# Shifted rows of the last image fetched between partitions of SBUF, second averages and bank copies moved up, and TensorE's results stored on SP's queue

## The chip, the cores and the metric

One core of one Trainium2 chip runs the whole program. Its engines work at the same time and meet through semaphores: TensorE (PE, with the weight loads PEld), VectorE (DVE), ScalarE (ACT), GpSimd (POOL) and SyncE (SP, which here only issues transfers). POOL issues transfers too. The metric is the device time of one execution, in microseconds (us); less is better.

## The reference, cut to what matters

The input is 16 images of 384 channels and 32 x 32 pixels, in float32. Layer 0 is attention over the 1024 pixels, layer 1 a 7 x 7 convolution of each channel by itself; both have a group normalization (32 groups of 12 channels, no affine) ahead of them and are added to their input.

```python
x = x + attention(gn(x), w_qkv, w_proj, b_proj)     # 8 heads of 48
w_sym = (w + rot90(w,1) + rot90(w,2) + rot90(w,3)) * 0.25
x = x + depthwise_conv7x7(gn(x), w_sym, pad=3)
def gn(v):                                          # per image, per group of 12 channels
    return (v - mean(v)) / sqrt(var(v) + 1e-5)
```

## The kernel before, in words

The channels lie on partitions in three tiles of 128 (`NK = 3`, index `k`). Image after image, TensorE makes q and k (line 489) and v (line 515), then per pair of heads the scores (560), whose exponentials ACT takes (568), and the sums over v (580), and the projection (641; for the last image in parts, 685). The result, with the residual, is x1. DVE does the convolution of the image before beside it, by folding (`fold_ops`, lines 771 to 876): it uses the left-right symmetry of the weights, so that it adds shifted copies (`sides`), collects them by row offset (`rows_e`, `rows_o`), and adds these to x1 in place.

Three of the 48 tiles of the convolution go to TensorE: `PE_TILES` are (14, 2), (15, 2) and (15, 1) (image, k). Only (15, 0), called `LAST`, is left to DVE at the end. A tile on TensorE goes through these steps:

- `conv_begin` (712): ACT copies x1 into xn with even and odd rows apart (line 725). For image 15 the values are not normalized yet: the scale is put in at the end and the shift comes in as a "border" term.
- `conv_store` (961): SP writes xn to `xd` in DRAM, two planes of 16 + 3 rows, with rows of zeros around them that POOL wrote once in `conv_prepare` (904, at about 500 us).
- `conv_load` (972): for each half `a` of the channels (64), SP issues four loads from `xd`; each fills one group of 16 channels with eight row-shifted copies each, 128 partitions in all (`sh`). `loads` (1459) says when.
- `conv_on_pe` (992): 7 taps by 4 groups of matmuls per half, into PSUM (`ps_conv`). The tap matrices are made on DVE from `wsh`, which POOL gathered in `conv_prepare`.
- `conv_take` (1019): ACT copies the bank to SBUF (`rows`, line 1022). `conv_perm` (1024): TensorE puts the rows back in channel order by two matmuls a half (1031, `ps_rows`); ACT copies out with the scale (1046; for image 14 without, 1050); POOL adds it to x1 by an accumulating transfer (1052), and the sum is stored (1054), on SP for half a tile and on POOL for a whole one.

The order of the work is written out by hand: a small planner keeps two clocks, `clock` for TensorE and `vclock` for DVE. `after(wait, cost, f)` puts DVE work in a queue of due times; `catch_up(t)` issues due work and taps of the folding until `vclock` is at `t`. Each engine then runs what it was given strictly in that order, and a wait holds everything behind it on that engine.

The end of the last image stands in `fast_finish` (1510) and `fast_end` (1534). After the last projection `fast_end` begins both TensorE tiles, lets ACT take the moments of the three channel tiles, and lets TensorE average them over groups in two steps: `st.average` of the means (line 363), then `spread_of` on DVE (374 to 376), then `st.average` of the squares, then `scale_of` (380 on DVE, and a power on POOL, 381), then `factors` (1578: `shift_of` on DVE, 384; nine activations for three border tiles on ACT, 1593; three accumulating transfers on POOL, 1596). From then on DVE can put the scale into `LAST` (line 804) and end it with two half stores on SP (880). Between these steps stand the pieces of TensorE's convolution, `pe_conv`.

At the program's end each engine loads a flag (`again`, 1677) and branches around a general version of the kernel that isn't needed (1678); then all meet in a barrier (1722).

Of the kernel before, what the change touches and what calls it, by code (L numbers as in the profile page):

```python
# [45 lines left out]
def kernel(  # L46
# [100 lines left out]
    def run(general):  # L147
        tag = "g" if general else "f"
        with ExitStack() as stack:
# [32 lines left out]
            def flat(t):  # L182
                return t.rearrange("p h n -> p (h n)")
# [521 lines left out]
            def by_rows(t):  # L705

                return t.rearrange("p (m q w) -> p q m w", q=2, w=W)
# [4 lines left out]
            def conv_begin(st, b, k, engine=None):  # L712
                name = f"xn1_{b}_{k}"
                if general:
                    xn1s[b, k] = npool.tile([P, N], F32, tag="xn1", name=name)
                elif b == B - 1:
                    xn1s[b, k] = flat(epool.tile([P, 2, HALF], F32, tag="e", name=name))
                else:
                    xn1s[b, k] = tpool.tile([P, N], F32, tag="t", name=name)
                if general:  # L720
                    st.apply(xn1s[b, k], x1s[b, k], k, engine)
                else:
                    dst = xn1s[b, k].rearrange("p (q m w) -> p q m w", q=2, w=W)
                    if b == B - 1:
                        nc.scalar.copy(dst, by_rows(x1s[b, k]))
                    else:
                        st.apply(dst, by_rows(x1s[b, k]), k)

            def conv_tap(b, k, dy, dx):
                (oy, iy), (ox, ix) = region(dy, dx)  # L730
# [10 lines left out]
            def grid(t):  # L741
                return t.rearrange("p (h w) -> p h w", w=W)
# [153 lines left out]
            NG = P // CG  # L896
            PLANE = (H // 2 + PAD) * W

            def inputs(i):

                first = (1 - i % 2) * RI // 2 + i // 2
                return slice(first, first + (CG - 1) * RI + 1, RI)

            def conv_prepare():
# [5 lines left out]
                with nc.allow_non_contiguous_dma(reason="small, once"):  # L910
                    nc.gpsimd.dma_start(
                        w_rows[:, :, KS : (KS + 1) * KS], wsym.rearrange("p k i j -> p k (i j)")
                    )
                    none = zero[:, 0 : NK * KS].rearrange("p (k t) -> p k t", k=NK)
                    nc.gpsimd.dma_start(w_rows[:, :, 0:KS], none)
                    nc.gpsimd.dma_start(w_rows[:, :, (KS + 1) * KS :], none)
                    for n, k in enumerate(PE_K):
                        for i in range(RI):
                            nc.gpsimd.dma_start(
                                wsh[inputs(i), n].rearrange("p g t d -> p g (t d)"),  # L920
                                bass.AP(
                                    w_d.tensor,
                                    w_d.offset + (k * P * (KS + 2) + i) * KS,
                                    [[(KS + 2) * KS, CG], [CG * (KS + 2) * KS, NG], [1, 2 * KS]],
                                ),
                            )
                for bk in PE_TILES:
                    xd = dconv.tile([P, 2 * PLANE], F32, tag=f"x_{len(xds)}", name=f"xd_{len(xds)}")
                    xds[bk] = xd

                    for lo, n in ((0, 1), (H // 2 + 1, 2), (H // 2 + 3, 2), (2 * PLANE // W - 1, 1)):
# [40 lines left out]
            def conv_load(b, k, a):  # L972

                t = qkpool.tile([P, 2, N], F32, tag="qk", name=f"sh_{b}_{k}_{a}")
                t = t.rearrange("p a n -> p (a n)").rearrange("p (g n) -> p g n", n=HALF)
                xd = xds[b, k]

                for i in range(NG // 2):
                    nc.sync.dma_start(
                        t[:, i],  # L980
                        bass.AP(
                            xd.tensor,
                            xd.offset + (a * NG // 2 + i) * CG * 2 * PLANE,
                            [[PLANE, 2 * CG], [W, RI // 2], [1, HALF]],
                        ),
                    )
                shs[b, k, a] = t


# [34 lines left out]
            def conv_perm(b, k, a):  # L1024
# [29 lines left out]
                queue.dma_start(  # L1054
                    out[b, k * P + part.start : k * P + part.stop].rearrange("p h w -> p (h w)"), dst
                )

            def exact_step(u, i):
# [406 lines left out]
            def conv_piece(rows=True):  # L1465
# [44 lines left out]
            def fast_finish(b):  # L1510
# [3 lines left out]
                for o in range(NK):  # L1514
# [19 lines left out]
            def fast_end(b):  # L1534
# [41 lines left out]
            ends = {}  # L1576
# [149 lines left out]
```

## Time and profile before

| | us |
|---|---|
| median of 3 runs | 2852.77 (2851.55 to 2854.41) |
| the profiled execution, its own time | 2858.37 |
| its span, first to last instruction | 2856.6 |
| PE busy in the span | 2831.3 (99%) |
| DVE, ACT, POOL busy | 2079.9, 1664.2, 264.1 |
| granted TensorE clock, mean | 0.995 |

The page has the busy time of each engine, forty slices of the span, the transfers by queue, the chain of work that ended last and the costliest groups of instructions. The trace behind it answers questions: the chain in order of time, who waited for whom in a stretch, the instructions of one line, and the busy time, the clock and the DMA rate of any stretch. Times in it count from the span's start. "A <- B" says that A waited for B; q after an engine's name is its sequencer.

### The profile page before, as it was taken

How to read it: one execution, taken by the hardware profiler on the slowest of the kernel's cores; microseconds unless marked ns; L12 is line 12 of the kernel's file. 1: busy time of each engine (PE TensorE's matmuls, PEld its weight loads, DVE VectorE, ACT ScalarE, POOL GpSimd, SP SyncE). 2: the span in 40 equal slices, each digit the busy share in tenths (PEclk: the TensorE clock that was granted, in tenths of full speed). 3: DMA queues.
4: the chain of work that ended last, by engine and by line, in shares of the span. 5: the costliest groups of instructions: out<-in, count | busy, mean ns of one | idle time of the engine just before them, and what ended most of it. 6: DMA issues, size and time to landing. Idle time of an engine off the chain costs nothing.

```text
span 2856.6 us, 46038 instructions
## 1 busy us (share of the span) xinstructions
PE 2831.3 (99%) x19342; PEld 1116.2 (39%) x19342; DVE 2079.9 (73%) x2261; ACT 1664.2 (58%) x1951; POOL 264.1 (9%) x418
## 2 busy tenths in 40 slices
PE   9999999999999999999999999999999999999996
PEld 5344343433434344343433434334343433434332
DVE  4503968959598695977959598595977959598786
ACT  2637647475574746647475574756647476574733
POOL 3201011310101001010010100001010010100001
PEclk9999999999999999999999999999999999999998
DMA  6622131211212112030211212112130121202225
GB/s 242 189 37 49 34 74 28 55 50 44 64 32 58 45 39 67 27 81 24 51 50 44 64 32 49 52 37 64 34 81 24 44 57 42 66 25 50 62 74 149
DMA packets 76153, 170.49 MB, mean 60 GB/s; under 512 B 31680, under 2 KB 33728, under 8 KB 74400
## 3 DMA queue, kind: packets, MB, share of 16 engines
q0 software_dynamic: 33360, 110.93, 15.2%
q1 hardware_dynamic: 42576, 56.52, 7.2%
q8 instruction: 154, 2.52, 0.4%
q14 instruction: 63, 0.52, 0.1%
HBM read 117.09 MB, written 28.68 MB: 51 GB/s over the span
## 4 chain that ended last, share of the span: by engine, by line
PE 97%; issue 1%; DMA 1%; POOL 0%; ACT 0%; SPq 0%; POOLq 0%; DVE 0%
PE ps_s L560 31%; PE acc L580 31%; PE ps_qk L489 17%; PE ps_v L515 9%; PE ps_proj L641 8%; PE warm L1396 0%; PE ps_proj_last L685 0%; PE ps_conv L1007 0%; DMA sh<-xd 0%; DMA x<-border 0%; DMA x<-conv 0%; PE ps_st_x L363 0%; POOL x L1052 0%; DMA xd<-xn 0%; PE ps_rows L1031 0%
## 5 line engine op out<-in xcount | busy, mean ns | idle before, releaser
L568 ACT ACTIVATE e<-ps_s 128x1024 f32<-128x1024 f32 x1024 | 1021.8, 1030 | 446.5 <-PE ps_s L560 445.2
L560 PE MATMUL ps_s<-qk 48*64 48x512 f32 x8192 | 1033.7, 589 | 0.0
L580 PE MATMUL acc<-e,v 64*64 64x512 f32 x8192 | 1033.0, 588 | 0.0
L780 DVE TENSOR_TENSOR side<-padded 128x1024 f32<-128x1024 f32 x270 | 329.3, 1220 | 339.4 <-ACT padded L751 339.3
L783 DVE SCALAR_TENSOR_TENSOR rows_e<-side,even,rows_e 128x1024 f32<-128x1024 f32 x405 | 509.7, 1274 | 85.7 <-ACT rows_e L762 84.1
L580 PEld LDWEIGHTS acc<-e,v 64*64 64x64 f32 x8192 | 307.0, 132 | 573.6 <-issue 573.4
L560 PEld LDWEIGHTS ps_s<-qk 48*64 48x64 f32 x8192 | 305.5, 132 | 576.8 <-issue 526.2
L489 PE MATMUL ps_qk<-x,wqk 128*128 128x512 f32 x1152 | 502.5, 595 | 0.0
L489 PEld LDWEIGHTS ps_qk<-x,wqk 128*128 128x128 f32 x1152 | 218.1, 190 | 277.8 <-issue 273.0
L799 DVE TENSOR_TENSOR x<-x,rows_e 128x992 f32<-128x992 f32 (+2 forms) x270 | 311.1, 1152 | 0.0
L799 DVE TENSOR_TENSOR x<-x,rows_o 128x928 f32<-128x928 f32 (+2 forms) x265 | 304.2, 1148 | 3.0
L496 ACT COPY qk<-ps_qk 128x1024 f32<-128x1024 f32 x96 | 97.2, 1012 | 318.5 <-PE ps_qk L489 318.5
L515 PE MATMUL ps_v<-wv,x 128*128 128x384 f32 x768 | 252.6, 486 | 0.0
L641 PE MATMUL ps_proj<-o,wp 128*128 128x512 f32 x540 | 234.2, 592 | 0.0
L535 ACT COPY v<-ps_v 64x384 f32<-64x384 f32 x256 | 121.6, 475 | 122.4 <-PE ps_v L515 119.8
L515 PEld LDWEIGHTS ps_v<-wv,x 128*128 128x128 f32 x768 | 145.9, 190 | 108.2 <-issue 14.3
L783 DVE SCALAR_TENSOR_TENSOR rows_o<-side,odd,rows_o 128x1024 f32<-128x1024 f32 x135 | 172.8, 1280 | 1.6
L783 DVE SCALAR_TENSOR_TENSOR x<-side,even,x 128x1024 f32<-128x1024 f32 x135 | 172.6, 1279 | 0.0
L886 POOL DMA_DIRECT2D out<-x x44 | 24.6, 558 | 1590.3 <-DVE x L799 1590.2
L641 PEld LDWEIGHTS ps_proj<-o,wp 128*128 128x128 f32 x540 | 102.6, 190 | 126.2 <-issue 117.7
L649 ACT ACTIVATE x<-ps_proj,bp 128x1024 f32<-128x1024 f32 x45 | 50.2, 1115 | 167.5 <-PE ps_proj L641 167.5
L762 ACT ACTIVATE rows_e<-padded,even 128x1024 f32<-128x1024 f32 x135 | 146.8, 1167 | 0.0
(165 smaller groups left out, 1044.5 us busy)
## 6 DMA issues: line engine op xcount, KB each, us to landing
x<-in_x POOLq DMA_DIRECT2D x90, 512.0 KB, 5.4
inv<-inv SPq DMA_DIRECT2D x126, 256.0 KB
out<-x POOLq DMA_DIRECT2D x46, 512.0 KB, 3.0
xs<-in_x POOLq DMA_DIRECT2D x42, 512.0 KB, 6.5
qk<-qk POOLq DMA_DIRECT2D x96, 128.0 KB, 4.1
sh<-xd SPq DMA_DIRECT2D x24, 256.0 KB
o<-o SPq DMA_DIRECT2D x180, 32.0 KB
x<-in_x SPq DMA_DIRECT2D x6, 512.0 KB
```

The costliest lines, as they stand in the source:

```text
L489: nc.tensor.matmul(ps[:, h, :], lhsT=wqk[:, k, s, t, :], rhs=xns[b][:, k, h * HALF : (h + 1) * HALF], start=(k == 0), stop=(k == NK - 1),)
L496: nc.scalar.copy(halves(qks[u][:, s, :]), ps)
L515: nc.tensor.matmul(ps[:, j, 0:C], lhsT=xns[b][:, k, t * P : (t + 1) * P], rhs=wv[:, k, :], start=(k == 0), stop=(k == NK - 1),)
L535: nc.scalar.copy(dst[:, :, 0 : HEADS // 2 * (D + 1)].rearrange("p k (h d) -> p k h d", d=D + 1)[:, :, :, 0:D], src.rearrange("p k (h d) -> ...
L560: nc.tensor.matmul(ps[64 * c : 64 * c + 64, a, :], lhsT=qk[r, 1, 64 * kb : 64 * kb + 64], rhs=qk[r, 0, h * HALF : (h + 1) * HALF], start=True,
L568: nc.scalar.activation(es[n], ps, AF.Exp, scale=SCALE)
L580: nc.tensor.matmul(accs[a][64 * j : 64 * j + 64, :], lhsT=v[rows, kb, c : c + 64], rhs=e[rows, j, :], start=(kb == 0), stop=(kb == 2 * NT ...
L641: nc.tensor.matmul(ps[:, h, :], lhsT=wp[:, t, o * P : (o + 1) * P], rhs=os_[b, t // 2][:, t % 2, h * HALF : (h + 1) * HALF], start=(t == 0 ...
L762: nc.scalar.activation(grid(rows_e[dy - 1]), padded_view(i), AF.Identity, scale=even[:, k, dy, 0:1],)
L780: vec.tensor_tensor(grid(sides[n]), padded_view(i, j), padded_view(i, -j), op)
L783: vec.scalar_tensor_tensor(dst, src, w, dst, ALU.mult, ALU.add)
L799: vec.tensor_tensor(dst, dst, src, op)
```

## The change

It acts on the convolution on TensorE and on the order of the work after the last attention.

- The copy of (15, 2) and (15, 1) goes into planes with rows of zeros inside SBUF (`late["planes", k]`, in the memory of `v`, which is no longer needed; POOL sets the zero rows by six memsets in `fast_finish`). ACT makes it in two copies of 512 columns instead of one of 1024. `conv_store` isn't called for image 15, and the two `xd` tensors of these tiles are gone.
- `conv_load` issues eight transfers a half instead of four, one for each row shift. For image 15 they go from the planes to `sh`, from SBUF to SBUF on SP; for (14, 2) from `xd` in DRAM, now on POOL. Channels lie in another order in `sh`, so the gather of `wsh` (32 transfers instead of 16) and `perm` are laid out to match. POOL's zero rows for `xd` are four transfers instead of twelve.
- `loads(2)` stands right behind the copies in `fast_end`, and another `loads(1)` ahead of the first piece of (15, 2).
- For image 15 ACT takes a bank right after its last tap, in `conv_piece`.
- In `fast_end` the second average stands one piece of convolution after the first (now four taps, before three taps and a permutation); the permutation of (14, 2) comes behind it. DVE's due times are 1.5, 1.5 and 4.0 instead of 2.5, 2.2 and 4.5.
- The last half tile (15, 1, a = 1) is added to x1 on DVE from PSUM (`conv_add`, two instructions of 64 x 512), not by ACT and an accumulating transfer.
- All stores of TensorE's tiles are issued on SP.

```diff
                 elif b == B - 1:
-                    xn1s[b, k] = flat(epool.tile([P, 2, HALF], F32, tag="e", name=name))
+                    xn1s[b, k] = late["planes", k]
+                    for q in range(2):
+                        nc.scalar.copy(
+                            grid(xn1s[b, k][:, (q + 1) * W + q * PLANE :][:, 0:HALF]),
+                            by_rows(x1s[b, k])[:, q],
+                        )
+                    return
...
+            NONE = ((0, 1), (H // 2 + 1, 4), (2 * PLANE // W - 1, 1))
...
-                            nc.gpsimd.dma_start(
-                                wsh[inputs(i), n].rearrange("p g t d -> p g (t d)"),
...
+                            for a in range(2):
+                                half = slice(a * NG // 2, (a + 1) * NG // 2)
+                                row = (KS + 2) * KS
+                                nc.gpsimd.dma_start(
+                                    wsh[inputs(i), n, half].rearrange("p g t d -> p g (t d)"),
...
-                for bk in PE_TILES:
+                for bk in PE_TILES[0:1]:
...
-                        perm[:, row].rearrange("p (g c) -> p g c", c=CG),
+                        perm[:, row].rearrange("p (c g) -> p g c", c=CG),
...
-                for i in range(NG // 2):
-                    nc.sync.dma_start(
-                        t[:, i],
...
+                half = slice(a * P // 2, (a + 1) * P // 2)
+                for i in range(RI):
+                    lo = (1 - i % 2) * PLANE + i // 2 * W
+                    if (b, k) in xds:
+                        nc.gpsimd.dma_start(t[inputs(i)], xds[b, k][half, lo : lo + HALF])
+                    else:
+                        nc.sync.dma_start(t[inputs(i)], xn1s[b, k][half, lo : lo + HALF])
                 shs[b, k, a] = t
...
+                if (b, k) == PE_TILES[-1] and a == 1:
+                    after(4.0, 1.5, lambda: conv_add(b, k, part))
+                    return
...
-                dst = x1s[b, k][part]
-                nc.gpsimd.dma_start(dst, t[part], accum_op=ALU.add)
-                queue = nc.sync if part.stop < P else nc.gpsimd
-                queue.dma_start(
-                    out[b, k * P + part.start : k * P + part.stop].rearrange("p h w -> p (h w)"), dst
+                nc.gpsimd.dma_start(x1s[b, k][part], t[part], accum_op=ALU.add)
+                store(b, k, part)
+
+            def conv_add(b, k, part):
+                s = ends["st"].sc[part, k, 0:1]
+                for q in range(2):
+                    dst = by_rows(x1s[b, k][part])[:, q]
+                    nc.vector.scalar_tensor_tensor(
+                        dst, grid(pss[b, k][part, q, :]), s, dst, ALU.mult, ALU.add
+                    )
+                store(b, k, part)
+
+            def store(b, k, part):
+                nc.sync.dma_start(
+                    out[b, k * P + part.start : k * P + part.stop].rearrange("p h w -> p (h w)"),
+                    x1s[b, k][part],
                 )
...
                 if last == KS:
                     loads(1)
+                    if b == B - 1:
+                        conv_take(b, k, a)
                     perms.append((b, k, a))
 
             def conv_rows():
-                for p in perms:
-                    conv_take(*p)
                 while perms:
...
                 check_vector()
+
+                planes = v.rearrange("p k c -> p (k c)")
+                for n, k in enumerate(PE_K):
+                    late["planes", k] = t = planes[:, n * 2 * PLANE : (n + 1) * 2 * PLANE]
+                    for lo, rows in NONE:
+                        nc.gpsimd.memset(t[:, lo * W : (lo + rows) * W], 0.0)
...
                     conv_begin(st, b, k)
-                    conv_store(b, k)
-                    pe_conv.extend(((b, k, 0, 0, KS), (b, k, 1, 0, 3), (b, k, 1, 3, KS)))
+                    pe_conv.extend(((b, k, 0, 0, KS), (b, k, 1, 0, 4), (b, k, 1, 4, KS)))
+                loads(2)
...
                     conv_piece(False)
+                for p in perms:
+                    conv_take(*p)
+                loads(1)
                 conv_piece(False)
                 catch_up(clock)
                 mean, var = st.first
                 st.average(late["masks"], 0, mean)
                 clock += 1.6
-                after(2.5, 0.6, lambda: st.spread_of(mean, var))
+                after(1.5, 0.6, lambda: st.spread_of(mean, var))
                 first = [perms.popleft() for _ in range(2)]
-                for p in first:
-                    conv_take(*p)
                 conv_piece(False)
-                for p in first:
-                    conv_perm(*p)
                 catch_up(clock)
                 st.average(late["masks"], NK, st.d)
                 clock += 1.6
-                after(2.2, 0.2, st.scale_of)
-                after(4.5, 0.4, lambda: factors(st))
+                after(1.5, 0.2, st.scale_of)
+                after(4.0, 0.4, lambda: factors(st))
+                for p in first:
+                    conv_perm(*p)
                 conv_piece(False)
-                catch_up(clock + 2.0)
+                catch_up(clock)
```

More of the change, by code (lines that the diff above doesn't have):

```diff
@@ L723, in conv_begin @@
                     dst = xn1s[b, k].rearrange("p (q m w) -> p q m w", q=2, w=W)
[L724 to L727, printed above, removed]
+                    st.apply(dst, by_rows(x1s[b, k]), k)
             def conv_tap(b, k, dy, dx):
@@ L918, in conv_prepare @@
                         for i in range(RI):
-                            nc.gpsimd.dma_start(
-                                wsh[inputs(i), n].rearrange("p g t d -> p g (t d)"),
[L921 to L926, printed above, removed]
-                for bk in PE_TILES:
+                            for a in range(2):
[3 more added lines that the diff above has]
+                                    wsh[inputs(i), n, half].rearrange("p g t d -> p g (t d)"),
+                                    bass.AP(
+                                        w_d.tensor,
+                                        w_d.offset + (k * P + a * P // 2) * row + i * KS,
+                                        [[NG // 2 * row, CG], [row, NG // 2], [1, 2 * KS]],
+                                    ),
+                                )
+                for bk in PE_TILES[0:1]:
                     xd = dconv.tile([P, 2 * PLANE], F32, tag=f"x_{len(xds)}", name=f"xd_{len(xds)}")
                     xds[bk] = xd
-                    for lo, n in ((0, 1), (H // 2 + 1, 2), (H // 2 + 3, 2), (2 * PLANE // W - 1, 1)):
+                    for lo, n in ((NONE[0], (NONE[1][0], 2), (NONE[1][0] + 2, 2), NONE[2])):
                         nc.gpsimd.dma_start(xd[:, lo * W : (lo + n) * W], zero[:, 0 : n * W])
@@ L975, in conv_load @@
                 t = t.rearrange("p a n -> p (a n)").rearrange("p (g n) -> p g n", n=HALF)
-                xd = xds[b, k]
-                for i in range(NG // 2):
-                    nc.sync.dma_start(
-                        t[:, i],
[L981 to L986, printed above, removed]
+                half = slice(a * P // 2, (a + 1) * P // 2)
[5 more added lines that the diff above has]
+                        nc.sync.dma_start(t[inputs(i)], xn1s[b, k][half, lo : lo + HALF])
                 shs[b, k, a] = t
@@ L1050, in conv_perm @@
                     nc.scalar.copy(by_rows(t), src)
-                dst = x1s[b, k][part]
-                nc.gpsimd.dma_start(dst, t[part], accum_op=ALU.add)
-                queue = nc.sync if part.stop < P else nc.gpsimd
-                queue.dma_start(
-                    out[b, k * P + part.start : k * P + part.stop].rearrange("p h w -> p (h w)"), dst
+                nc.gpsimd.dma_start(x1s[b, k][part], t[part], accum_op=ALU.add)
[6 more added lines that the diff above has]
+                        dst, grid(pss[b, k][part, q, :]), s, dst, ALU.mult, ALU.add
+                    )
+                store(b, k, part)
[3 more added lines that the diff above has]
+                    x1s[b, k][part],
                 )
```

## The prediction

> **What bounds the kernel now.** I read the page first, then the chain in order of time, the waits after 2770 us, the clock by stretches, and the last instructions.
>
> ```profile
> PE 2831.3 (99%) x19342; PEld 1116.2 (39%) x19342; DVE 2079.9 (73%) x2261; ACT 1664.2 (58%) x1951; POOL 264.1 (9%) x418
> ...
> PE 97%; issue 1%; DMA 1%; POOL 0%; ACT 0%; SPq 0%; POOLq 0%; DVE 0%
> ```
>
> TensorE sets the time up to the last image's projection, and nothing of the change touches its order there. So only the end can move. The chain in order of time (start, length, what), from the copies of x1 on:
>
> ```profile
> 2785.34 2.79 DMA xd<-xn
> ...
> 2790.13 6.48 DMA sh<-xd
> ...
> 2796.65 7.58 PE ps_conv L1007 x48
> ...
> 2811.70 5.78 DMA x<-conv
> ...
> 2822.75 6.15 DMA x<-border
> ...
> 2830.90 4.49 issue
> ...
> 2836.85 3.53 issue
> ...
> 2841.20 4.52 issue
> ```
>
> Here transfers carry the end. The three "issue" pieces are POOL waiting for a landed sum before it may store it, then for ACT, then for the last sum. The waits between 2770 and 2858 us (total, times, longest):
>
> ```profile
> POOL out L1054 <- DMA x<-conv: 14.2, 3, 5.2
> ...
> PE ps_rows L1031 <- ACT rows L1022: 4.0, 2, 3.3
> DVE d_x L374 <- PE ps_st_x L363: 3.1, 1, 3.1
> DVE sc_x L384 <- POOL sc_x L381: 2.5, 1, 2.5
> ...
> PE ps_conv L1007 <- DMA sh<-xd: 2.2, 1, 2.2
> ...
> DVE x L804 <- DMA rest<-border: 0.8, 1, 0.8
> ```
>
> TensorE's two gaps cost twice: the stretch after each ran at half clock (by stretch: busy time of each engine, then as the last three figures clock, DMA share and GB/s).
>
> ```profile
> 2797.95:2801.37 3.42, 3.42 (x24) 1.04 (x20) 3.42 (x4) 2.13 (x6) 0.00 (x0) 0.50 1.00 331
> ...
> 2825.26:2828.67 3.41, 3.41 (x11) 0.76 (x11) 2.57 (x3) 0.35 (x1) 0.00 (x0) 0.50 1.02 192
> ```
>
> DVE ends at 2836.83, TensorE at 2838.90. The rest is closing. By line, the instructions of SP's stores, of the branch and of the barrier:
>
> ```profile
> L880 SPq DMA_DIRECT2D out<-x x2: 1448/1654/1860, 2841.9 to 2843.8; - x2
> ...
> L1678 POOLq COMPARE_BRANCH  x1: 58/58/58, 2846.7 to 2846.7; - x1
> L1678 POOLq INC_SWDGE_SEM  x1: 1196/1196/1196, 2850.4 to 2850.4; - x1
> ...
> L1722 POOLq DRAIN  x3: 50/98/4152, 2851.6 to 2856.3; - x3
> ```
>
> POOL closes last: store issued 2845.73 to 2846.29, branch 2846.7, first instruction behind it 2849.9, 1.2 us, a drain of 4.15, barrier, end at 2856.6: 10.3 us behind its store. SP branches at 2845.3 and is at work again at 2848.6.
>
> [...] the accumulating half tiles moved 94 GB/s at DMA share 1.00 (2841.6 to 2844.4), the trace shows no plain copy from half the partitions to another place in SBUF. [...]
>
> **The change part by part.**
>
> *Early work.* `conv_prepare`: 16 more gathers, 8 fewer zero rows, at 0.53 us each: 4.2 us on POOL, which ends there at 521.3 and next has work at 530.8. Nothing, with 9.5 us of cover. The 16 loads of (14, 2), 0.55 to 0.9 us each on POOL, come near 2713 and 2723 where POOL waits from 2716.7 to 2770.9; their matmuls start at 2776.3. A store of (14, 0) may issue some us later; nobody waits. Nothing; without cover up to 14 us. SP loses 8 issues there. The six memsets fall behind 2771.4, before ACT's copies at 2784.3.
>
> *First wait.* Two ACT copies of 512 columns, by the 0.58 us of a bank copy (128 x 512), end at about 2785.4 like the one of 1.05. Gone: the store to DRAM, 2.79 us. SP then issues 8 loads instead of 4. Not shown before; the nearest are the old loads at 0.60 us (0.51 to 0.99, twice the bytes), 0.65 with the gap. Low end 0.5, high end the 1.86 of a half store. I take 0.65: 8 x 0.65 = 5.2, issued by 2790.6; landing about 2 us later, 2792.6. [...] TensorE is done with (14, 2) at 2794.5, so its wait of 2.17 goes, and with it 1.55 of half clock (7.58 against 6.03 for 56 records, by 32 in 3.46 at full clock elsewhere). (15, 2, 0) ends at 2800.55 instead of 2804.2. All 32 loads take 32 x 0.65 = 21 us, to 2806.2; the last half is needed at 2819.8.
>
> *Averages.* First average 1.65: 2802.2. DVE comes to `spread_of` one tap (1.1) earlier, at 2801.8, and waits about 0.5 instead of 3.1; done 2802.8. TensorE: four taps 3.45 (2805.65), second average 1.65 (2807.3), the permutation 1.9 (2809.2). The power on POOL stands behind the accumulating transfer of (14, 2): ACT copy 1.0 (2810.3), 0.3, issue 0.88 (2811.5), power 0.91: 2812.4. Before, the power also stood behind a store that waited 5.2 us; it ended at 2819.25. So the factors come 6.8 us sooner. DVE gets there after six taps, at 2810, and waits 2.5.
>
> *DVE's end.* From `spread_of` to its last tap DVE worked 30.4 - 2.45 - 0.84 = 27.1 us; with the moved tap 28.2. So 2802.8 + 28.2 + 2.5 = 2833.5. The border term lands near 2820 and is used at 2823: no wait. Then `conv_add`: two instructions, by the 0.74 us of the 128 x 512 sum from PSUM (line 699), 1.45: 2834.95.
>
> *TensorE's end.* 2809.2, three taps 2.6 (2811.8), (15, 1, 0) 6.05 (2817.9), permutation 1.9 without wait or half clock, since the banks are taken (2819.8; was 2828.2), four taps 3.45, permutation 1.9, three taps 2.6 (2827.75), bank copy and permutation 2.65: 2830.4 instead of 2838.9. It is ahead of DVE.
>
> *Sums and stores.* Three border transfers from 2814.5 on land as before 5 to 7 us after issue, (15, 2) is summed at about 2823 to 2829, its half of (15, 1) at 2826.5 to 2832, each landing followed by a store on SP that waits there: SP's order is (14, 2), (15, 2), (15, 1, 0), the two halves of `LAST`, (15, 1, 1). The last three wait for DVE at 2832.8, 2833.5 and 2835. What is late next, if the sum of (15, 1, 0) lands after 2833, is all three. The last is issued by 2835.6 at 0.6 each; the 1.45 and 1.86 of before came while a half tile was being accumulated, which is over then. With those prices it is 2836.7.
>
> *Closing.* SP branches at 2835.6, 3.3 us, eight plus twelve waits 1.4, barrier and end 0.8: 2841.1. POOL's last issue is at 2827.4, and with the landing of that sum (2832) ahead of the 1.2 and 4.15 its closing is over at 2837.7, so the drain of 4.15 leaves the path.
>
> Sum against the profiled span: 2841.1 - 2856.6 = -15.5 us. The profiled execution's own time, 2858.37, is 1.77 above its span and 5.6 (0.2%) above the median; I carry the difference over: 2852.77 - 15.5 = 2837.3.
>
> **Rivals.**
>
> 1. *The closing stays with POOL.* If POOL's closing starts only after the last store's issue, as now, the end lies 10.3 behind that: 2835.6 + 10.3 = 2845.9, -10.7: 2842.1. For: the drain is the last thing in the trace. Against: nothing links it to SP.
> 2. *The first loads land late.* The first matmul needs all eight now, not one of four. Landing at 2797 leaves the wait and the half clock: (15, 2, 0) ends at 2804.6, 4.0 later, DVE's wait at `spread_of` grows by as much and moves all behind it: 2845.1, so 2841.3. For: in the old kernel the fourth load took 6.48 us. Against: that one stood behind two stores and three other loads, this one behind seven loads of half the size.
> 3. *Slower: copies inside SBUF are dear.* With d us per load on SP, the last lands at 2785.4 + 32d + 2, and behind it lie 8.0 of taps and permutation, 2.65, 1.55, 0.7 and 5.5 of closing: the span ends at 2805.8 + 32d. At d = 0.65 this doesn't bind; from 1.10 it sets the end, from 1.59 it is slower than before, from 1.77 by over 0.2%. At the 1.86 of the half store it gives 2865.3, so 2861.5. [...] Against: old loads moved 300 GB/s (2788 to 2791) at 0.60 us[...].
> 4. *It doesn't move.* DVE is still held by the power, or several small delays add up; d near 1.6: 2852.
>
> **How the numbers follow.** Forecast 0.63; rival 1 0.12; rival 2 0.12 (with the other delays of a few us); rival 3 0.08 in all, of which 0.06 over the 0.2%; rival 4 0.03, and 0.02 for gains under 0.2%. 0.2% is about 5.7 us, what a measurement of this kernel can tell from none: faster means under 2847.1. Faster 0.63 + 0.12 + 0.12 + 0.02 = 0.89 (the 0.02 of rival 3 below 1.59 counts as same); same 0.05; slower 0.06. Low end: DVE without any wait ends 3.0 sooner, 2834.3, less run noise 2834.0; the high end takes in rivals 1 and 2 with 1.1 for dear half stores and run noise, 2845.
>
> **What would show it.** No TensorE gap before the first (15, 2) matmul and no half clock until 2830; loads at 0.5 to 0.7 us each; power done near 2812; `LAST` done near 2833.5, the sum from PSUM behind it; POOL's drain over before SP's last store lands. Wrong it is if loads cost over 1.1 us, the power stays behind 2815, or the drain still comes last.

## The result: 11 us faster, and the profile after

The changed kernel takes 2842.75 us (median of 7 runs, 2841.55 to 2846.19), the kernel before beside it 2853.82 (7 runs, 2851.20 to 2857.96): a ratio of 0.9962 [0.9951, 0.9974], 11.1 us less. The forecast was 2837.3 in a range of 2834 to 2845, 15.5 us less.

The profiled execution of the changed kernel took 2846.19 us with a span of 2844.1. From its page, busy time and the chain that ended last:

```profile
PE 2828.3 (99%) x19342; PEld 1117.4 (39%) x19342; DVE 2081.4 (73%) x2263; ACT 1663.4 (58%) x1952; POOL 268.6 (9%) x444
...
DVE 0%; issue 0%; DVEq 0%
```

In what the view could follow of the chain, back to 2824.3, only DVE stands; TensorE and transfers have left it. Its last pieces in order of time (start, length, what) are the end of `LAST` and the sum from PSUM:

```profile
2833.54 0.66 DVE x L800
2834.20 0.20 DVEq L1701
2834.40 0.15 DVE x L800
2834.55 0.34 issue
2834.89 1.43 DVE x L1064 x2
```

The view of the chain leaves out the issuing of transfers, and there is one more step on SP. DVE is done at 2836.32, SP's last store is issued from 2837.86 to 2838.36. Its queue is late because the store of (15, 1)'s first half waits there until 2834.6 for its landed sum, and the two half stores of `LAST` come behind it. The first line is from SP's own waits between 2825 and 2845 us, the others from the engines' waits between 2772 and 2846 us (total, times, longest):

```profile
SPq L1070 <- DMA x<-conv: 15.6, 2, 14.0
...
DVE sc_x L384 <- POOL sc_x L381: 1.7, 1, 1.7
...
PE ps_rows L1034 <- ACT rows L1025: 0.7, 1, 0.7
```

There is no wait of TensorE for `sh` and none of DVE for `ps_st_x`. POOL no longer waits for a landed sum to store it; that wait now stands on SP. What POOL still waits for is hidden in this view: its queue stands from 2818.6 to 2824.3 and from 2824.8 to 2828.5 (the line of L1057 below) until two border transfers have landed, ahead of the sums into the same tiles. This execution's end lies 2.8 us later in time than that of the forecast's profile; the two stretches of time that ran at half clock there are at full clock here (columns as before; clock, DMA share and GB/s last):

```profile
2797.95:2801.37 3.42, 3.42 (x40) 1.01 (x32) 3.38 (x4) 3.36 (x10) 0.00 (x0) 1.00 0.43 147
...
2825.26:2828.67 3.41, 3.14 (x26) 0.68 (x24) 3.38 (x4) 1.31 (x2) 0.41 (x1) 1.00 1.02 193
```

Half clock comes only at 2833.9, behind TensorE's last matmul (2831.0). By line, the instructions of SP's loads and stores, of POOL's waits ahead of its sums, of POOL's drain, and SP's first instructions behind the branch (times one by one in ns, then first and last start):

```profile
L989 SPq DMA_DIRECT2D sh<-v x32: 531/595/1446, 2788.2 to 2809.9; - x32
...
L883 SPq DMA_DIRECT2D out<-x x2: 532/1163/1794, 2835.4 to 2836.0; - x2
...
L1057 POOLq EVENT_SEMAPHORE  x2: 3659/4702/5746, 2818.6 to 2824.8; - x2
...
L1746 POOLq DRAIN  x3: 50/98/4111, 2836.1 to 2843.8; - x3
...
L1702 SPq EVENT_SEMAPHORE  x8: 17/17/17, 2841.9 to 2842.4; - x8
```

The loads cost 0.70 us each (21.7 us between the first and the 32nd). POOL's long drain runs from 2836.05 to 2840.16, and SP comes out of its branch only at 2841.9: the closing is on SP, and POOL's lies beside it.

For what follows, "the end" is the time from the start of the last matmul of line 685 (the last projection) to the span's end; this leaves out what happened earlier. It was 72.05 us in the profile that the forecast was made from and is 56.78 here: 15.27 less, where 15.5 was forecast. Yet the median of the runs moved by 11.1. The experiments first ask where those four microseconds are, then what each part of the change is worth.

### The profile page after: what moved, and what is told of

It reads as the page before. It is cut to its first block, busy times and chain, and to the rows that moved or that the text cites. A ratio compares the mean times of both kernels' runs of the same rounds, so it can differ in the third digit from the quotient of the medians.

```text
span 2844.1 us, 46108 instructions
## 1 busy us (share of the span) xinstructions
PE 2828.3 (99%) x19342; PEld 1117.4 (39%) x19342; DVE 2081.4 (73%) x2263; ACT 1663.4 (58%) x1952; POOL 268.6 (9%) x444
## 5 line engine op out<-in xcount | busy, mean ns | idle before, releaser
L515 PEld LDWEIGHTS ps_v<-wv,x 128*128 128x128 f32 x768 | 145.9, 190 | 108.2 <-issue 14.3
```

The source lines that it names most:

```text
L515: nc.tensor.matmul(ps[:, j, 0:C], lhsT=xns[b][:, k, t * P : (t + 1) * P], rhs=wv[:, k, :], start=(k == 0), stop=(k == NK - 1),)
```

## The experiments

Ends and marks in us from the start of the last matmul of line 685, one profiled execution each (DVE and SP: end of their last work; SP's closing left out):

| kernel | first average starts | DVE | SP | span's end |
|---|---|---|---|---|
| before, first profile | 19.64 | 52.31 | 60.75 | 72.05 |
| before, second | 16.61 | 48.98 | 57.40 | 68.41 |
| before, third | 15.94 | 48.75 | 56.99 | 68.19 |
| before, fourth | 16.48 | 48.11 | 55.45 | 67.13 |
| changed, first | 14.48 | 49.00 | 51.05 | 56.78 |
| changed, second | 14.48 | 49.00 | 50.35 | 55.83 |

**The kernel before, again.** No edit.

> The kernel before, once more. Measured from the last matmul of line 685 to the end, its profiled execution took 72.05 us and the changed kernel 56.78: 15.3 less, as forecast, while the medians differ by only 11. Theory A [...]: the two half-clock stretches in the profiled end (1.55 + 1.9 us) are not in every execution; another profile shows an end of 68.5 to 70.5 us with one of them or none, and times spread in steps of about 1.7 us. Theory B (the change made the part before the end slower): the end is again near 72, and the missing 4 us must lie ahead of it.

2858.77 us (13 runs) against 2857.83 (23): 1.0004 [0.9996, 1.0013]. The end was 68.41 us, 3.6 shorter than in the first profile and 0.09 below the range of theory A. TensorE's weight loads waited for `sh` twice, 1.8 us together (3.1 in one wait in the first profile, where the matmuls stood still for 2.17), and the stretch behind was at full clock. Two further executions of the same kernel were profiled at the close to learn which end is usual.

> The kernel before as it is, one look. Two profiles of its end so far gave 72.05 us (TensorE's first gap one wait of 2.17 us, and the stretch behind it at half clock) and 68.41 (the gap in two waits of about 1 us, no half clock behind it). If the long end is usual, this look gives 71 to 73 and a half-clock stretch near 14 us behind the last matmul of line 685; if it is the rarer one, 67.5 to 69.5 without. The forecast's sum was made against the long end; the medians (11 us) fit the short one.

> The same again, for the same question: which of the two ends of the kernel before is usual. 71 to 73 with a half-clock stretch behind the first gap, or 67.5 to 69.5 without.

2854.57 and 2852.02 us (one run each; the kernel before beside them 2857.72), ends of 68.19 and 67.13, the second 0.4 below the range named. So the long end is one of four. In all four the first load of (15, 2) is issued 3.7 us after the mark and the next seven at the same times to 0.02 us; in the first profile alone TensorE then stands still for 2.17 us, in the others its matmuls pause for less than 0.15 us there. The loads landed later in that execution, and why stays open. The waits of the fourth profile from 2775 to 2855 us:

```profile
PE ps_rows L1031 <- ACT rows L1022: 3.0, 2, 2.3
...
PEld ps_conv L1007 <- DMA sh<-xd: 1.7, 2, 1.1
```

and its clock over the whole of TensorE's end (columns as above):

```profile
2796.00:2831.00 35.00, 32.02 (x249) 11.38 (x242) 32.55 (x36) 12.33 (x22) 7.15 (x9) 1.00 0.58 143
```

Here the second gap of 2.3 us cost no half clock at all, whereas the 2.17 us of the first profile did. The second and the third profile have a gap of 3.1 and 3.4 us there, and one half-clock stretch of 3.4 us behind it.

Where the clock changes can be read in the traces. In the first profiles of both kernels every stretch between two changes lasts a whole multiple of 3.413 us, to 0.01 us (3.41, 23.89, 3.41 and 13.65 us from 2797.95 on in that of before). With the time laid off in such steps from the trace's first clock entry, the step ahead of the first profile's half-clock stretch, then the two that hold the fourth profile's gap (columns as above):

```profile
2794.54:2797.95 3.41, 1.30 (x16) 0.56 (x20) 3.38 (x4) 3.35 (x8) 0.00 (x0) 1.00 0.98 329
...
2813.81:2817.22 3.41, 2.67 (x28) 0.65 (x20) 3.38 (x5) 3.39 (x8) 1.30 (x2) 1.00 0.21 84
2817.22:2820.63 3.41, 1.87 (x8) 0.71 (x8) 2.67 (x3) 1.97 (x4) 1.66 (x2) 1.00 1.02 192
```

In the first, TensorE worked for 1.30 of 3.41 us, and the next 3.41 ran at half clock; ahead of the same profile's second half-clock stretch it had worked for 0.87 (2821.84 to 2825.26). In the fourth, the border between two steps cuts the gap into 0.74 and 1.54 us; 2.67 and 1.87 us of work are left, and the clock stays full. So in these executions half clock went with how much work the gap left in one step, and not with the gap's length alone. At what amount of work it sets in was not measured, and these few cases don't show a rule.

**The kernel before, with TensorE kept busy in both gaps.**

```diff
+            def keep_warm(dst, n):
+                m = late["masks"].rearrange("p b c -> p (b c)")
+                for _ in range(n):
+                    nc.tensor.matmul(dst, lhsT=m[:, 0:P], rhs=m[:, 0:HALF], start=True, stop=True)
...
+                if (b, k, a, first) == (B - 1, PE_K[0], 0, 0):
+                    keep_warm(dst, 2)
...
+                    if (b, k) == (B - 1, PE_K[0]):
+                        keep_warm(pss[b, k][:, 0, :], 3)
```

> The kernel before with two idle matmuls ahead of the first taps of (15, 2) and three ahead of its permutation, into banks that the next matmul clears, so that TensorE's two gaps are filled; nothing is left out. The two profiles of the kernel before took 72.05 us for the end with two half-clock stretches in it and 68.41 with one. If the half clock is what differs: no such stretch until TensorE's last matmul and an end of 66 to 67.5 us. If something else differs between the two profiles: the end stays at 68.4 or more.

2855.41 us against 2858.58: 0.9992 [0.9984, 1.0]. There was no half clock before 2838, and yet the end was 68.73 us, no shorter than the usual one. The idle matmuls took more than the gap: the first average started at 18.28 instead of about 16.5. TensorE ended 0.7 us earlier than in the second profile, POOL's and SP's work at the same time as there (58.22 and 57.32 us against 58.11 and 57.40), with 14.3 us of POOL's waits for landed sums. What TensorE won behind the second gap a transfer took back: POOL's sum of (15, 2) waited 4.4 us for a landed border transfer, where it had waited for ACT in the second profile. How much of that the later average caused isn't separated, and the test can't price the first gap, since its fillers cost what they saved.

**The changed kernel, again.** No edit.

> The changed kernel as it is, a second time, on the chip of the following run. My theory: its end (from the start of the last matmul of line 685 to the span's end) has no TensorE gap of over 1 us, [...] and it repeats at 56.78 us within 0.7, where that of the kernel before gave 72.05 and 68.41 in two executions. The ratio to the kernel before is then 0.9955 to 0.9968 (10 to 13 us). The rival, that the 56.78 was as much a chance as the 72.05, expects an end of 59 or more, or a half-clock stretch after the last projection.

2842.94 us against 2853.62: 0.9966 [0.9952, 0.9979]. The end was 55.83; TensorE's, DVE's, ACT's and POOL's work ended at the same 43.73, 49.00, 41.74 and 42.5 us as in the first profile, and the clock was full to TensorE's last matmul. That is 0.25 below the range named, by 0.7 us of one store on SP (below). What was a chance is the long end of before; that of the changed kernel repeats in its two profiles. In the second, TensorE worked for 31.30 of the 32 us from 2795 to 2827; its longest gap is 0.70 us. Between the two profiles of the changed kernel lie 4.9 us of span, and 3.9 of them had passed by the last projection: the first matmul for q and k of image 1 starts at 177.6 in one and 173.7 in the other, behind 10.2 and 3.4 us of half clock at the start (11.1 to 21.4 and 13.8 to 17.2 us).

**Only the rows of image 15 through DRAM again.** All else stays as changed, with eight loads a half.

```diff
-                    xn1s[b, k] = late["planes", k]
-                    for q in range(2):
-                        nc.scalar.copy(...)
+                    xn1s[b, k] = flat(epool.tile([P, 2, HALF], F32, tag="e", name=name))
+                    dst = xn1s[b, k].rearrange("p (q m w) -> p q m w", q=2, w=W)
+                    nc.scalar.copy(dst, by_rows(x1s[b, k]))
...
-                for bk in PE_TILES[0:1]:
+                for bk in PE_TILES:
...
-                        nc.sync.dma_start(t[inputs(i)], xn1s[b, k][half, lo : lo + HALF])
+                    queue = nc.gpsimd if b < B - 1 else nc.sync
+                    queue.dma_start(t[inputs(i)], xds[b, k][half, lo : lo + HALF])
...
+                    conv_store(b, k)
```

> The changed kernel, but the shifted rows of image 15 go through DRAM again (store, then eight loads a half). If the fetch inside SBUF is what took the first wait away: TensorE waits 2 to 3 us for the first loads again, perhaps with a half-clock window behind it, and the end is 2 to 4.5 us longer than the 56.8 of the changed kernel. If the fetch is hidden either way and the other edits carry the gain: within 0.7 us of it.

2850.58 us, 0.9966 [0.9954, 0.9978]; end 61.63, 4.9 to 5.8 us longer than the changed kernel's two, more than the 2 to 4.5 expected. The waits from 2787 to 2851 us bring back what was forecast to go:

```profile
PE ps_conv L1005 <- DVE x L783: 2.4, 1, 2.4
DVE d_x L374 <- PE ps_st_x L363: 2.3, 1, 2.3
```

(The profile names a DVE line as TensorE's releaser; the matmuls that wait are the first of (15, 2), and the only new work ahead of them is the store to DRAM and the loads from it: the first load is issued 3.69 us after the mark, as in the kernel before, where the changed kernel issues it at 0.91.) A half-clock stretch follows at 2801.2. The first average starts 4.3 us later, and DVE ends 4.3 us later. The fetch inside SBUF thus takes the first wait away. The timed ratio doesn't separate this kernel from the changed one, nor do those of the next two experiments; the traces do, though the half-clock stretch takes part in the one execution that the 4.9 rests on.

**Only the order of the end as before:** three taps, permutation, second average, four taps.

```diff
-                    pe_conv.extend(((b, k, 0, 0, KS), (b, k, 1, 0, 4), (b, k, 1, 4, KS)))
+                    pe_conv.extend(((b, k, 0, 0, KS), (b, k, 1, 0, 3), (b, k, 1, 3, KS)))
...
-                after(1.5, 0.6, lambda: st.spread_of(mean, var))
+                after(2.5, 0.6, lambda: st.spread_of(mean, var))
...
+                for p in first:
+                    conv_perm(*p)
...
-                after(1.5, 0.2, st.scale_of)
-                after(4.0, 0.4, lambda: factors(st))
-                for p in first:
-                    conv_perm(*p)
+                after(2.2, 0.2, st.scale_of)
+                after(4.5, 0.4, lambda: factors(st))
...
-                catch_up(clock)
+                catch_up(clock + 2.0)
```

> The changed kernel with the order of before around the second average (three taps, permutation of (14, 2), second average, four taps; due times 2.5, 2.2, 4.5). If earlier averages shorten the end: the factors come 2 to 3 us later and the end is 1 to 3 us longer. By the forecast's own sums it may go the other way: VectorE has work while the power is under way, its wait of 1.7 us goes, its last tap comes 1 to 2.5 us sooner, and the end is 0.5 to 2.5 us shorter than 56.8.

2849.63 us, 0.9971 [0.9960, 0.9982]; end 58.45, 1.7 to 2.6 us more than the changed kernel's two. DVE ends at the same time to 0.05 us (48.95): it waits less for the power, 0.8 instead of 1.7, and 0.9 for the border instead. The power itself took more than twice as long, from this kernel's instructions of line 381:

```profile
L381 POOL TENSOR_TENSOR sc_x<-d_x,mhalf x1: 2845/2845/2845, 2814.3 to 2814.3; 128x3 f32<-128x3 f32 x1
```

against 1.20 us in the changed kernel. It ended 3.6 us later, and with it the border transfers, the sums behind them, and SP's last store (52.29 against 51.05). So in these executions the earlier average pays through the transfers, not through DVE as the sum had it. Why the power took 2.85 us stays open, and so does what the earlier average is worth without that.

**Only the last half tile by ACT and an accumulating transfer again,** without the sum from PSUM on DVE.

```diff
-                if (b, k) == PE_TILES[-1] and a == 1:
-                    after(4.0, 1.5, lambda: conv_add(b, k, part))
-                    return
```

> The changed kernel, but the last half tile is again scaled by ScalarE and added by an accumulating transfer, then stored on SP. Forecast: that transfer lands about 7 us behind TensorE's last permutation, SP's last store and GpSimd's closing come behind it, and the end is 1.5 to 3.5 us longer than 56.8. Rival: VectorE sets the end, is freed of 1.45 us, and the end is about 1 us shorter.

2850.11 us, 0.9967 [0.9953, 0.9980]; end 59.04, 2.3 to 3.2 more. DVE ends 1.5 sooner, but POOL can issue the last sum only at 2835.07, and SP's last store waits for its landing until 2840.9. That store is only 0.5 to 1.2 us later than in the changed kernel. The larger part is POOL's closing, which comes last again: its long drain runs from 2843.56, behind the landing, to 2847.75, while SP is ready for the barrier at 2845.9. So here the accumulating transfer that landed last kept the closing with POOL, for 4.19 us of drain, just as the last store did in the kernel before (4.15).

**Only the stores of TensorE's whole tiles on POOL again.**

```diff
-                nc.sync.dma_start(
+                queue = nc.sync if part.stop < P else nc.gpsimd
+                queue.dma_start(
```

> The changed kernel, but the stores of TensorE's tiles stand on GpSimd's queue again where they did before. Forecast: the store of (14, 2) waits there for its landed sum and holds the power behind it by 4 to 5 us, VectorE waits for the factors by as much, and the last store opens GpSimd's closing of 10 us only then: 6 to 9 us longer than the 56.8 of the changed kernel (from the last matmul of line 685 to the end). Rival: [...] the end moves by less than 1 us.

2855.52 us, 0.9993 [0.9984, 1.0002]: no gain that can be told from none is left. (As in the kernel before, the second half of (15, 1) goes to POOL too, since its `part` ends at partition 128.) The end is 65.25, 8.5 to 9.4 us more, in the fastest of the twelve executions; against the usual ends of before, 67.1 to 68.4, 2 to 3 us remain. POOL in order of time (start, length, line, tiles, the idle time before and what ended it):

```profile
2812.99 0.55 POOL L1071 DMA_DIRECT2D out<-x  x1 [3.98 <-DMA x<-conv]
2813.55 0.91 POOL L381 TENSOR_TENSOR sc_x<-d_x,mhalf 128x3 f32<-128x3 f32 x1
...
2837.44 0.56 POOL L1071 DMA_DIRECT2D out<-x  x1 [4.01 <-DVE x L1064]
```

The first store waits 3.98 us for its sum and holds the power back; DVE's wait for it grows to 6.3, its end to 53.53. The last store stands on POOL at 2837.44, and the span ends 10.9 us behind it. The issue of one such store costs 0.34 to 0.53 us on SP in the changed kernel and 0.55 to 0.57 on POOL here, so the 8.5 us are something else: the last store is over 3.3 us later, behind a DVE that ends 4.5 later for the waits in POOL's order, and the closing behind it is 5.1 us longer on POOL than on SP.

**The loads halved:** 64 loads of 64 KB instead of 32 of 128 KB, the same bytes.

```diff
-                        nc.sync.dma_start(t[inputs(i)], xn1s[b, k][half, lo : lo + HALF])
+                        for c in range(2):
+                            n = HALF // 2
+                            nc.sync.dma_start(
+                                t[inputs(i)][:, :, c * n : (c + 1) * n],
+                                xn1s[b, k][half, lo + c * n : lo + (c + 1) * n],
+                            )
```

> The changed kernel with each of the 32 loads inside SBUF cut in two, so 64 loads of 64 KB on SP. Measured spacing of the 32 was 0.70 us. If issue on SP sets the pace (0.6 to 0.7 us a load whatever its size), the loads take 40 to 45 us, TensorE waits at every half tile, and by the line of the forecast (last issue + 2 + 18.4) the end is 5 to 9 us longer than 56.8. If bytes set it (0.35 us a load), no change over 1 us.

2870.05 us, 1.0042 [1.0027, 1.0057]: slower than before. The end is 77.78, 21 us more than the changed kernel's, far beyond the expectation. TensorE's wait and the loads (two views of this kernel):

```profile
PE ps_conv L1015 <- DMA sh<-v: 17.4, 3, 11.3
```

```profile
L991 SPq DMA_DIRECT2D sh<-v x64: 531/592/1792, 2788.0 to 2838.1; - x64
```

A load of half the size costs the same to issue, 0.59 us in the median and 0.81 with what lies between; the 64 take 51.8 us. What the expectation had left out is the half clock: stretches of 3.4, 6.8 and 13.7 us begin at 2799, 2809 and 2833, and the longest matmul of the taps took 1.06 us where the median was 0.58. So between 128 and 64 KB a load, on this path, the time of the loads went with their number (21.7 us for 32, 51.8 for 64) and not with the bytes.

**ACT takes three first products of `LAST`,** which then is stored in one transfer; an attempt at a faster version, by way of DVE's part of the chain.

```diff
-                        (ts, lambda dy=dy, j=j, n=n: first(rows_o[n % 2], sides[slot[j]], o(dy, j)))
+                        (
+                            0.02 if (b, k) == LAST else ts,
+                            lambda dy=dy, j=j, n=n: (on_act if (b, k) == LAST else first)(
+                                rows_o[n % 2], sides[slot[j]], o(dy, j)
+                            ),
+                        )
...
-                                    half_store(b, k, half),
+                                    half and last_store(b, k),
```

> The changed kernel with two more edits: LAST is stored by one transfer instead of two halves, and its three first products of the odd rows (0.75 us each on VectorE) go to ScalarE. If VectorE and then SP's queue set the end: VectorE is done 1.5 to 2.2 us sooner, SP has one store of 1.8 us less ahead of its last one, and the end is 2 to 4 us shorter than 56.8. If ScalarE's order makes VectorE wait for its products, or TensorE is next: less than 1 us.

2847.79 us, 0.9962 [0.9950, 0.9975]; end 58.13, 1.4 to 2.3 us longer instead of 2 to 4 shorter. The waits from 2786 to 2850 us say why:

```profile
ACT rows_o L792 <- DVE x L803: 5.2, 1, 5.2
...
PE ps_rows L1041 <- ACT rows L1032: 3.9, 1, 3.9
...
DVE rows_o L786 <- ACT rows_o L792: 2.8, 1, 2.8
```

A product on ACT waits 5.2 us for the buffer that DVE still reads, and behind it on ACT stands the bank copy that TensorE needs. DVE waits for ACT in turn.

**`LAST` in one store,** on the chip of the changed kernel's second profile.

```diff
-                                    half_store(b, k, half),
+                                    half and last_store(b, k),
...
-            def half_store(b, k, h):
-                c = slice(h * HALF, (h + 1) * HALF)
+            def last_store(b, k):
...
-                    out[b, k * P : (k + 1) * P].rearrange("p h w -> p (h w)")[:, c], x1s[b, k][:, c]
+                    out[b, k * P : (k + 1) * P].rearrange("p h w -> p (h w)"), x1s[b, k]
```

> LAST is stored by one transfer of 512 KB behind its second half's last tap, instead of two halves of 256 KB. In the changed kernel the second half store held SP's queue for 1.79 us (2835.98 to 2837.77), and the last store stands behind it. My theory: the 1.79 belongs to the issue of a second transfer of LAST directly behind the first, so that with one of about 0.6 us, issued at about 2834.9 and so done before the sum from PSUM is there (2836.3), the last store goes out at about 2836.4 instead of 2837.86: the end is 55.3 us instead of 56.78, 1 to 1.5 less, ratio 0.0004 to 0.0005 below the changed kernel's in the run before this one. The rival, that SP's queue was full [...] and any transfer in that place takes as long, expects the 1.8 in the one store and an end of 56.5 to 57.5.

2842.73 us, 0.9960 [0.9946, 0.9973], and the changed kernel beside it 2842.94: no difference that can be told. The one store took 0.46 us and the last store was issued by 49.53 us, 0.8 to 1.5 sooner: the dear second half store is gone. The end is 55.82 all the same. What took its place is in the waits of SP's own queue from 2825 to 2845 us:

```profile
SPq L1701 <- SPq L1701: 4.1, 2, 3.1
```

In the changed kernel's second profile the same line is one wait of 3.2 us, the branch. Here there are two, 3.1 and about 1.0: the second ends when the last store has landed, at 2838.67, 4.9 us after its issue began and behind a transfer of 512 KB. In the changed kernel's second profile it landed in 3.6 us, before SP was out of its branch. The first theory held for the issue, not for the end; in this execution the landing of the last transfer bounds it. Neither attempt beats the changed kernel.

## Why the prediction was right in its mechanism and 4 us off in its size

Marks are in us from the last matmul of line 685; in the forecast's profile that is 2784.52.

1. *Nothing moves before the end.* Nothing of the change shows there. But that matmul starts between 2783.1 and 2790.9 in the six profiles of the two kernels, so a sum over the end says nothing about one execution's span, and a shift of a microsecond ahead of it isn't excluded.
2. *The first wait goes, and its half clock.* It did, and putting DRAM back brings both again. The loads cost 0.70 us, not 0.65; that they land about 2 us after their issue was the author's estimate, and the trace doesn't show the landing, only that TensorE had no wait for it. (15, 2, 0) ended at 14.5 where 16.0 was forecast; 0.6 of this is that six of its 56 matmuls had run before the wait (50 records behind it), which the 6.03 us counted again; the other 0.9 wasn't taken apart.
3. *Averages, power, DVE.* The power ended at 26.3 (27.9 forecast), DVE waited 1.7 for it (2.5) and not at all at `spread_of` (0.5). `LAST` was done at 47.5 (49.0), the sum from PSUM cost 1.43 (1.45). The worth of the earlier average was put in the wrong place: undone, it costs nothing on DVE, but 1.2 to 1.9 us on the last store, with a power that took 2.85 us for a reason not found.
4. *TensorE's end:* 43.7 (45.9), one gap of 0.7, no half clock.
5. *SP's last store:* issued by 51.05, where 51.1 was forecast. This is luck, since two errors cancel: DVE was 1.4 early, and the second half store took 1.79 us, not 0.6. The text named this price of before, but put it down to the accumulation beside it; that was wrong, since none is under way here. In the second profile it took 1.11. Why it is dear stays open.
6. *Closing on SP.* Branch 3.4, waits 1.4, barrier and end 0.8, as said; POOL's drain is over at 2840.16, before SP leaves its branch. The stores on SP are the largest part of the change, 8.5 us; undone alone, the parts cost 4.9, 1.7, 2.3 and 8.5 us against the first profile, each in one execution. Together that is 17.3, more than the whole. That they share waits, DVE's for the power and POOL's closing, is the likely reason. The bank copies moved up and the loads of (14, 2) on POOL were not undone alone.

**The step that failed** is the sum's base. The end of the changed kernel came out as the sum has it, 56.8 and 55.8 us where 2841.1 - 2784.5 = 56.6 was forecast. But it was set against one execution, "Sum against the profiled span", whose difference of 5.6 us to the median was carried over unchanged. That execution was long because of its end: three others of the same kernel end 67.1 to 68.4 us after the last projection, not 72.05. The mis-sized term is "its wait of 2.17 goes, and with it 1.55 of half clock": this wait and this half clock were there in one profile of four. In the other three the first average starts at 15.9 to 16.6, against 14.5 after the change: 1.5 to 2.1 us are to be had there, not the 3.7 of the text, and against the forecast's own execution it was even 5.2. From the usual end, 68.2, to 56.8 or 55.8 is 11.4 to 12.4 us. Off this goes 0.3: the time around the span grew from 1.77 us to 2.1. That leaves 11.1 to 12.1, and the medians moved by 11.1 and 10.7. So the gain is 4.4 us smaller than forecast. The changed kernel's median lies 5.45 above the forecast one, because the median of before also rose by 1.05, from 2852.77 in three runs to 2853.82 in seven.

Rivals 1 and 2 named 2842.1 and 2841.3 us, both nearer to the measured 2842.75 than the forecast. That is chance: neither mechanism happened, and the difference comes from the base. Rival 2, late first loads, didn't happen: TensorE has no wait for `sh`. Nor did rival 4: DVE's wait for the power is down to 1.7 us. Rival 3, dear loads, didn't happen at 0.70 us, but its mechanism is real: the halved loads, 1.62 us for each 128 KB, stand just above the 1.59 where its formula turns slower, which makes 1 us of span. The formula gives an end of 2805.8 + 32 x 1.62 - 2784.5 = 73.1 us; 77.78 was measured. Of the 4.7 missing, 2.4 are half clock: the four taps behind the last wait took 5.90 us instead of 3.48. The rest is SP's last store, delayed by its queue, and a longer closing. With these terms the turning point lies lower than 1.59; where was not measured.

## What to carry to other kernels

Ahead of a forecast, ask which costs of the profiled execution are there by chance: a late landing was one here (TensorE stood still for 2.17 us in one profile of four), and 3.4 us of half clock behind it another. A profiled time above the median is a reason to look for them, but doesn't say where: in the changed kernel's first profile, 3.4 above its median, the end was the usual one. A second profile of the unchanged kernel would have shown it (an end of 68.41 us against 72.05). A store that waits for a transfer belongs on a queue where nothing that matters stands behind it: on POOL's, one that waited 3.98 us held the power back. The engine whose transfer lands last can be the one that closes last, as POOL was here with 4.19 us of drain behind its last sum. Count issues as well as bytes before splitting a transfer: 64 loads of 64 KB took 51.8 us here, 32 of 128 KB 21.7.

## What the runs showed that was not expected

- A gap of TensorE of 2.17 us was followed by 3.4 us at half clock, one of 2.3 us in another execution of the same kernel by none. The first left 1.30 us of work in one step of 3.41 us, the other was cut by a border between two steps and left 2.67 and 1.87.
- At the program's start the half-clock stretch was 10.2 us long in one execution of the changed kernel and 3.4 in the other; the first matmul of image 1 started between 173.4 and 181.2 us in the six profiles of the two kernels. The latest had a second stretch of 6.8 us at half clock, from 155.0.
- The same 128 x 3 power on POOL took 0.91, 1.20 and 2.85 us in kernels that differ in the order of the work around it.
- A transfer from SBUF to SBUF of 64 KB cost SP as much to issue as one of 128 KB (0.59 and 0.60 us in the median); single ones took 1.4 to 1.8.
